# Filler work placed around the first scores and their maxima, divisions one cell later, one cell less for each cross-attention

## The chip, the core and the metric

The kernel runs on one core of a Trainium2 chip. A core has five engines with in-order queues of their own: TensorE (PE; its weight loads are listed as PEld), VectorE (DVE), ScalarE (ACT), GpSimd (POOL) and SyncE (SP, which here only issues DMAs). They meet through semaphores. The metric is the device time of one execution in microseconds (us), lower is better. A second number that matters for TensorE is the clock that it was granted, which the profile gives as a share of full speed.

## What is computed

Two transformer blocks on x, 2 sequences of 1024 tokens with 256 features, all in float32. Heads are 16 wide, 16 of them.

```python
q = ln(x);  x = x + mha(q, q)                 # layer 0: self-attention with biases
x = x + mha(ln(x), ln(ctx))                   # cross-attention to 64 context tokens
h = ln(x); top-2 of 8 experts, gates = softmax # mixture of experts, 1024 hidden units
x = x + sum_k gate_k * expert_k(h)
x = x + sa(ln(x))                             # layer 1: self-attention
x = x + ca(ln(x), ctx, mask)                  # masked cross-attention
x = x + fc2(gelu(fc1(ln(x))))                 # feed-forward
```

## The kernel before

**Cells.** Self-attention of a layer is cut into 128 cells (2 sequences, 2 halves of the queries, 4 groups of 4 heads, 8 blocks of keys; line 899). A cell works on four heads at a time, each in its own 32 rows of the array. It makes two kinds of scores. The "a" scores (L747) have the queries on the partitions and serve only to find each row's maximum (VectorE's reduction, L754). The "b" scores (L758) have the keys on the partitions, with the maximum already folded into the moving operand QB; ScalarE takes their exponential (L764), and `product` (L809) multiplies them with the values, some cells later, for one or two cells at once. ScalarE copies the product out of PSUM into one of two `part` buffers (L821), and POOL adds it to `acc` (L822; VectorE does in the last ten cells, where there are no more maxima). The a scores run `LEAD` = 10 cells ahead. After eight of them `collect` (L782) gathers the maxima, and `largest` transposes them (L702) and subtracts them from the queries (L704, the QB of the group).

**The first ten cells.** In layer 0 nothing precedes the a scores of cells 0 to 9, so they stand alone (`early`, L769), and other work is taken in between. `fill_up(cell, most)` (L784) takes steps from the planner until their cost is used up; `owed` grows by an amount after each early cell and is spent in the same way. Steps that are there to be taken are values (`values`, L594 and the copy L601), keys and queries of the next heads (`project_heads`, L624 and L631, whose rows then travel by DMA, L640), the folded biases (`fold_bias`, L452 to L456, copied by L581 and added to x by POOL, L418) and the context's keys and values (`context_task`: statistics, roots on POOL, centering L346, transposes L358, projections L975 and L997). In layer 1 the early cells are mixed with expert work.

**The planner.** `Stream` holds tasks as generators. A yielded positive number is a cost in us of TensorE; a number at or below zero is a wait, which in the cells is rounded up to whole cells of `CELL` = 2.9 us by setting the task's `first` (L145). Among tasks that may go, the one with the earliest due cell goes. When the cells are over, `rest` (L176) issues what is left, by rank, on a clock of its own that starts at 0, and its table `ready` of when each task may go on starts empty.

**After a pair of head groups.** `finish` sends the sums and the products to DRAM, `gather` fetches the products back, one cell later VectorE inverts the sums (L486) and one DMA writes them out, two cells later another DMA spreads them (L489), three cells later `divide` multiplies (L497, on POOL while there are a scores, else on VectorE), and for the second pair the projection (L426, L434) is added to the stream a cell after that. A quarter of the tokens is a unit; its projection starts a chain of cross-attention (`cross_tasks`: norm, `weigh`, `share`) and, in layer 0, the dispatch to the experts (`dispatch_task`: statistics L332, roots, centering L1255, transposes L358, router L1268, top-2 on VectorE). Expert slots (`slot`, L1592 and L1622) that are known by then fill the rest of layer 0. In `weigh`, as long as there are a scores, scores (SC), maxima (LA), transposes with exponentials (TU), products (PR) and division (DI) are set out by hand over cells (L1170), each line of the list being one cell. Else a second list is used.

PSUM has eight banks, handed out in turn (`bank`, L228), each given back when the engine that drains it has been issued.

Of the kernel before, what the change touches and what calls it, by code (L numbers as in the profile page):

```python
# [61 lines left out]
LEAD = 10  # L62
# [66 lines left out]
class Stream:  # L129
# [46 lines left out]
    def rest(self, later, cell, mark=None):  # L176

        now, ready = 0.0, {}  # L180
        while (self.tasks or later) and (mark is None or mark not in self.made):
            for c in sorted(later):
                if (c - cell) * CELL <= now:
                    for go in later.pop(c):
                        go()
            tasks = [t for t in self.tasks if self.made.issuperset(t.after)]
            able = [t for t in tasks if ready.get(t, 0.0) <= now]
            if able:
                t = max(able, key=lambda t: (t.rank, -ready.get(t, 0.0)))
                cost = self.advance(t)  # L190
                if cost is not None:
                    now += max(0.0, cost)
                    ready[t] = now - min(0.0, cost)
            else:
                now = min([ready[t] for t in tasks] + [(c - cell) * CELL for c in later])
        return now
# [3 lines left out]
def two_blocks(  # L200
# [314 lines left out]
    def self_attention(layer, tail, heads, arrive, extra, when_ready, beside=None):  # L515
# [30 lines left out]
        def at_cell(cell, go):  # L546
            later.setdefault(cell, []).append(go)
# [160 lines left out]
        def finish(h, cell):  # L708
# [11 lines left out]
            if g % 2 == 1:  # L720
                by = opool.tile([P, 512], F32, tag="by", name=f"by_{names}{h}", bufs=1)
                gather(n, dst)
                at_cell(cell + 1, lambda: invert(n, sm))
                at_cell(cell + 2, lambda: spread_out(n, by))
                at_cell(cell + 3, lambda: divide(dst, by))
                if g == 3:
                    at_cell(cell + 4, lambda: project(b, qh))

        def project(b, qh):
            def go():  # L730
# [148 lines left out]
        add_values(1, 34, [("norm", 1)] + (["filled"] if layer == 0 else []))  # L879
        if layer == 0:  # L880

            fill_up(-LEAD, 2.0)
            owed = 0.0
            for ahead in range(0, LEAD, 2):
                cell = now[0] = ahead - LEAD
                for n, _ in enumerate(early(ahead)):
                    for go in later.pop(cell + n, []):
                        go()
                    if (ahead, n) == (6, 1):
                        collect(0)  # L890
                        stream.add(largest(0), 0.75, last=cell, mark=("QB", 0))
                        fill_up(cell, 1.0)
                        stream.until(("QB", 0))

                    owed += 0.7
                    while owed > 0.6 and (cost := stream.step(cell)):
                        owed -= cost
        owed = 0.0
# [143 lines left out]
    def weigh(layer, b, pool, w, name, held):  # L1042
# [124 lines left out]
        SC, LA, TU, PR, DI = scores, largest, weights_turned, product, divided  # L1167
        if maxima[0]:

            for now in (  # L1170
                ((SC, 0, 0), (LA, 0, 0)),
                ((LA, 0, 1),),
                ((SC, 0, 1), (LA, 0, 2)),
                ((TU, 0, 0), (LA, 0, 3)),
                ((SC, 1, 0), (LA, 1, 0)),
                ((TU, 0, 1), (LA, 1, 1)),
                ((PR, 0),),
                ((SC, 1, 1), (LA, 1, 2)),
                ((TU, 1, 0), (LA, 1, 3)),
                ((DI, 0),),  # L1180
                ((TU, 1, 1),),
                ((PR, 1),),
            ):
                for step, *args in now:
                    step(*args)
                us = {SC: cost, TU: 1.15, PR: 1.1, DI: 0.55}.get(now[0][0])
                if us:
                    yield us
                yield 0.0
            return  # L1190
        for step, *args, wait in (
            (SC, 0, 0, None),
# [886 lines left out]
```

## Time and profile before

| | us |
|---|---|
| three timed runs | 1633.61, 1641.87, 1643.48 (median 1641.87) |
| profiled execution | 1630.99 |
| its span, first to last instruction | 1629.2 |
| PE busy in the span | 1581.6 |
| DVE, ACT, POOL busy in the span | 982.0, 912.3, 415.0 |
| mean granted TensorE clock | 0.980 |

The profile is one execution, and its line numbers are those of the kernel before. A row of the timeline gives start, length, engine, line, operation, what is written and what is read, how many instructions were merged (float32 matmuls are recorded twice each), and in brackets how long the engine had been idle and what ended that. A row of waits gives who waited for whom, total, number of times, longest. A row of windows gives the busy time of each engine in a stretch, then the clock, the DMA share and GB/s. A busy PE can also be a matmul that is waiting in the pipeline, since the ends of matmuls are modelled.

A few groups, for scale:

| line, engine, what | count | mean ns |
|---|---|---|
| L754 DVE, maximum of a 128x512 block | 1024 | 682 |
| L764 ACT, exponential of 128x512 | 1024 | 607 |
| L747 PE, a scores | 2048 | 634 |
| L758 PE, b scores | 2048 | 621 |
| L822 POOL, sum of 128x512 | 143 | 1271 |
| L821 ACT, copy of 128x512 | 157 | 597 |

### The profile page before, as it was taken

The numbers are of one execution on the slowest core, as the hardware profiler recorded it, in microseconds if no ns is written. First come the engines' busy times: TensorE is split into PE (matmuls) and PEld (weight loads), VectorE is DVE, ScalarE is ACT, GpSimd is POOL, SyncE is SP. The second block draws the span as 40 slices with busy tenths as digits, with TensorE's granted clock in tenths as the row PEclk, the third lists the DMA queues.
The fourth block names the chain that finished last, engine by engine and source line by source line (L and its number), as shares of the span: only waits on it lengthen the run. The fifth ranks groups of instructions, "written<-read, shape, count | busy, mean of one in ns | idle before, by whom it ended". The sixth has DMA issues, their size and how long they took to land.

```text
span 1629.2 us, 28274 instructions
## 1 busy us (share of the span) xinstructions
PE 1581.6 (97%) x10682; PEld 871.1 (53%) x10682; DVE 982.0 (60%) x2092; ACT 912.3 (56%) x1768; POOL 415.0 (25%) x549
## 2 busy tenths in 40 slices
PE   7999999999999988999999999999999999999998
PEld 3333344444443445788888753344444435536766
DVE  5687857688787737531114467876776877755400
ACT  2376867667665763433322327876776676674321
POOL 2134324234433403041112032411322323321010
PEclk8899999999997998999999999999999999999999
DMA  4333510110100215186566321000110002000000
GB/s 143 124 132 114 180 37 21 27 32 28 36 21 21 67 57 195 62 283 216 175 204 241 92 67 33 24 26 17 36 40 21 21 14 83 15 14 21 14 13 26
DMA packets 56591, 122.09 MB, mean 75 GB/s; under 512 B 12546, under 2 KB 26756, under 8 KB 56068
## 3 DMA queue, kind: packets, MB, share of 16 engines
q1 hardware_dynamic: 52612, 110.08, 20.9%
q0 software_dynamic: 3456, 9.51, 1.6%
q8 instruction: 86, 1.41, 0.4%
q10 hardware_dynamic: 384, 0.66, 0.2%
q14 instruction: 53, 0.43, 0.1%
HBM read 72.14 MB, written 39.42 MB: 68 GB/s over the span
## 4 chain that ended last, share of the span: by engine, by line
PE 91%; DVE 6%; issue 1%; DMA 1%; ACT 1%; POOL 0%; SPq 0%; DVEq 0%; POOLq 0%; ACTq 0%
PE banks L758 17%; PE banks L747 15%; PE banks L809 14%; PE banks L1592 8%; PE banks L1622 8%; PE banks L624 4%; PE banks L1764 3%; PE banks L1752 3%; PE banks L426 3%; PE banks L1051 2%; PE banks L594 2%; PE banks L1081 2%; PE banks L1117 2%; DVE mx_s L754 2%; PE banks L358 1%
## 5 line engine op out<-in xcount | busy, mean ns | idle before, releaser
L754 DVE TENSOR_REDUCE mx_s<-banks 128x1 f32<-128x512 f32 x1024 | 634.6, 682 | 209.3 <-PE banks L747 204.1
L764 ACT ACTIVATE pt_s<-banks 128x512 f32<-128x512 f32 x1024 | 531.2, 607 | 153.0 <-PE banks L747 127.5
L747 PE MATMUL banks<-KS,QS 16*128 16x512 f32 x2048 | 537.6, 634 | 3.5 <-issue 1.9
L758 PE MATMUL banks<-qb_s,KS 32*128 32x512 f32 x2048 | 511.7, 621 | 7.5 <-DVE qb_s L704 4.2
L822 POOL TENSOR_TENSOR acc_s<-acc_s,part_s 128x512 f32<-128x512 f32 x143 | 181.8, 1271 | 426.0 <-ACT part_s L821 414.0
L758 PEld LDWEIGHTS banks<-qb_s,KS 32*128 32x128 f32 x2048 | 177.8, 186 | 181.4 <-DVE mx_s L754 104.4
L809 PE MATMUL banks<-pt_s,v_s 128*20 128x512 f32 x2048 | 262.3, 605 | 0.7 <-DVE sc_c L1102 0.5
L747 PEld LDWEIGHTS banks<-KS,QS 16*128 16x128 f32 x2048 | 198.6, 187 | 77.2 <-issue 37.1
L1622 PE MATMUL banks<-w_slot,h_s 128*128 128x256 f32 x640 | 143.1, 380 | 0.0
L809 PEld LDWEIGHTS banks<-pt_s,v_s 128*20 128x20 f32 x2048 | 42.5, 98 | 181.2 <-ACT pt_s L764 128.9
L1622 PEld LDWEIGHTS banks<-w_slot,h_s 128*128 128x128 f32 x640 | 120.7, 190 | 19.8 <-DVE mx_s L754 1.5
L821 ACT COPY part_s<-banks 128x512 f32<-128x512 f32 x157 | 93.7, 597 | 62.0 <-PE banks L809 51.5
L1631 DVE SCALAR_TENSOR_TENSOR ys<-banks,gate,b 128x256 f32<-128x256 f32 x40 | 19.3, 483 | 162.8 <-PE banks L1622 161.6
L1598 ACT ACTIVATE h_s<-banks,w_slot 128x256 f32<-128x256 f32 x104 | 43.7, 471 | 119.3 <-issue 65.7
L1637 POOL DMA_INDIRECT results<-ys,to x40 | 38.6, 964 | 252.9 <-DVE ys L1631 169.3
L1592 PE MATMUL banks<-xsT,w_slot 128*128 128x256 f32 x416 | 95.7, 381 | 0.7 <-ACT xsT L365 0.7
L1592 PEld LDWEIGHTS banks<-xsT,w_slot 128*128 128x128 f32 x416 | 77.3, 190 | 14.8 <-DVE mx_s L754 2.3
L624 PE MATMUL banks<-xT_s,w_att 128*128 128x512 f32 x128 | 68.6, 672 | 0.0
L1755 ACT ACTIVATE h_f<-banks,w_ff 128x512 f32<-128x512 f32 x32 | 22.0, 687 | 73.9 <-PE banks L1752 73.9
L1102 POOL TENSOR_TENSOR sc_c<-sc_c,mx_c 128x512 f32<-128x512 f32 x38 | 39.5, 1042 | 76.9 <-DVE mx_c L1101 76.9
L1764 PE MATMUL banks<-w_ff,h_f 128*128 128x256 f32 x256 | 57.3, 380 | 0.0
L1752 PE MATMUL banks<-hT_f,w_ff 128*128 128x512 f32 x128 | 56.3, 593 | 0.0
(260 smaller groups left out, 1609.6 us busy)
## 6 DMA issues: line engine op xcount, KB each, us to landing
w_slot<-in_ff_w_dram SPq DMA_DIRECT2D x40, 576.0 KB
sorted_rows<-fill SPq DMA_DIRECT2D x36, 520.0 KB
w_slot<-in_ff_w_dram SPq DMA_DIRECT2D x26, 514.0 KB
whole<-acc_s SPq DMA_DIRECT2D x32, 256.0 KB
spare<-in_ff_w_dram SPq DMA_DIRECT2D x14, 514.0 KB
xs<-sorted_rows SPq DMA_DIRECT2D x20, 260.0 KB
ot_s<-whole SPq DMA_DIRECT2D x16, 256.0 KB
by_s<-turns SPq DMA_DIRECT2D x16, 256.0 KB
```

Source lines behind the costliest of these rows:

```text
L624: nc.tensor.matmul(p, lhsT=w[:, at + k * D + pair * P : at + k * D + (pair + 1) * P], rhs=xT[b][:, k, blk * 512 : (blk + 1) * 512], start= ...
L747: nc.tensor.matmul(sc, lhsT=QS[h % 4][r, qc * P : (qc + 1) * P], rhs=K[r, kh * 512 : (kh + 1) * 512], start=True, stop=True,)
L754: return i, lambda: nc.vector.tensor_reduce(mx[h][:, qc, j, kh : kh + 1], sc, AX.X, ALU.max)
L758: nc.tensor.matmul(sc, lhsT=K[r, n * P : (n + 1) * P], rhs=QB[h][r, :], start=True, stop=True)
L764: nc.scalar.activation(pt, sc, AF.Exp, scale=SCALE)
L809: nc.tensor.matmul(o[32 * j : 32 * j + VW, :], lhsT=V[b][:, cell % 8, 4 * g + j, :], rhs=exps.pop((cell, j)), start=(cell == cells[0]), st ...
L821: nc.scalar.copy(part, o)
L822: helper().tensor_tensor(acc[h], acc[h], part, ALU.add)
L1592: nc.tensor.matmul(ph[:, n, :], lhsT=w[:, at : at + P], rhs=xT[:, k, :], start=(k == 0), stop=(k == 1),)
L1622: nc.tensor.matmul(py, lhsT=h1[:, f, h * P : (h + 1) * P], rhs=w[:, f * D : (f + 1) * D], start=(f == 0), stop=(f == 7),)
L1752: nc.tensor.matmul(ph, lhsT=w1[:, at : at + P], rhs=hT[:, k, :], start=(k == 0), stop=(k == 1))
L1764: nc.tensor.matmul(py[:, n, :], lhsT=h1[:, f, t * P : (t + 1) * P], rhs=w2[:, f * D : (f + 1) * D], start=(f == 0), stop=(f == 7),)
```

## The change

Five edits. The table `ready` of `rest` starts from each task's `first`, so that a wait begun in the cells goes on in the rest. The division comes four cells after `finish` instead of three while there are a scores, and the projection after it moves along. Before the first score, steps worth 4 us are taken instead of 2; after each early cell 1.4 us are owed instead of 0.7; and after the first `collect`, up to 3 us of steps are taken ahead of the transposes of the maxima, and up to 1 us behind them. The hand-set list of `weigh` has eleven entries instead of twelve: the second scores of the second group come ahead of the first product, one maximum goes beside the product, and the first division beside the last transposes. Its cost is the sum over the entry's steps instead of the first step's alone, and if the a scores have ended while it runs, the waits written in the list are used instead of a cell.

```diff
-        now, ready = 0.0, {}
+        now, ready = 0.0, {t: (t.first - cell) * CELL for t in self.tasks}
...
-                at_cell(cell + 3, lambda: divide(dst, by))
+
+                late = 3 + maxima[0]
+                at_cell(cell + late, lambda: divide(dst, by))
                 if g == 3:
-                    at_cell(cell + 4, lambda: project(b, qh))
+                    at_cell(cell + late + 1, lambda: project(b, qh))
...
-            fill_up(-LEAD, 2.0)
+            fill_up(-LEAD, 4.0)
             owed = 0.0
             for ahead in range(0, LEAD, 2):
                 cell = now[0] = ahead - LEAD
...
                     if (ahead, n) == (6, 1):
                         collect(0)
+                        fill_up(cell, 3.0)
                         stream.add(largest(0), 0.75, last=cell, mark=("QB", 0))
+                        stream.until(("QB", 0))
                         fill_up(cell, 1.0)
-                        stream.until(("QB", 0))
-
-                    owed += 0.7
+
+                    owed += 1.4
                     while owed > 0.6 and (cost := stream.step(cell)):
                         owed -= cost
...
-            for now in (
-                ((SC, 0, 0), (LA, 0, 0)),
-                ((LA, 0, 1),),
-                ((SC, 0, 1), (LA, 0, 2)),
-                ((TU, 0, 0), (LA, 0, 3)),
-                ((SC, 1, 0), (LA, 1, 0)),
-                ((TU, 0, 1), (LA, 1, 1)),
-                ((PR, 0),),
-                ((SC, 1, 1), (LA, 1, 2)),
-                ((TU, 1, 0), (LA, 1, 3)),
-                ((DI, 0),),
-                ((TU, 1, 1),),
-                ((PR, 1),),
-            ):
+            for now, wait in (
+                (((SC, 0, 0), (LA, 0, 0)), 0.0),
+                (((LA, 0, 1),), 0.0),
+                (((SC, 0, 1), (LA, 0, 2)), 0.0),
+                (((TU, 0, 0), (LA, 0, 3)), 0.0),
+                (((SC, 1, 0), (LA, 1, 0)), 0.0),
+                (((TU, 0, 1), (LA, 1, 1)), 0.0),
+                (((SC, 1, 1), (LA, 1, 2)), 0.0),
+                (((PR, 0), (LA, 1, 3)), -1.5),
+                (((TU, 1, 0),), None),
+                (((DI, 0), (TU, 1, 1)), -1.4),
+                (((PR, 1),), None),
+            ):
                 for step, *args in now:
                     step(*args)
-                us = {SC: cost, TU: 1.15, PR: 1.1, DI: 0.55}.get(now[0][0])
+                us = sum({SC: cost, TU: 1.15, PR: 1.1, DI: 0.55}.get(step[0], 0.0) for step in now)
                 if us:
                     yield us
-                yield 0.0
+                if maxima[0]:
+                    yield 0.0
+                elif wait is not None:
+                    yield wait
```

## The prediction

> **What bounds the kernel now.** The page comes first: TensorE is busy for 97% of the span and the chain that ended last is 91% PE. So only two things can shorten the run: TensorE's idle time, and time in which its clock is granted at less than full. The span times (1 - 0.980), its mean clock, is 32.6 us; idle is 1629.2 - 1581.6 = 47.6 us.
>
> ```profile
> PE 1581.6 (97%) x10682; PEld 871.1 (53%) x10682; DVE 982.0 (60%) x2092; ACT 912.3 (56%) x1768; POOL 415.0 (25%) x549
> PE 91%; DVE 6%; issue 1%; DMA 1%; ACT 1%; POOL 0%; SPq 0%; DVEq 0%; POOLq 0%; ACTq 0%
> ```
>
> Next the windows, to find where both lie (columns: window, length, busy time of PE, PEld, DVE, ACT, POOL, then the clock):
>
> ```profile
> 20.00:30.00 10.00, 8.10 (x29) 4.84 (x32) 2.48 (x4) 1.22 (x3) 0.00 (x0) 0.83 0.35 67
> 30.00:40.00 10.00, 10.00 (x36) 3.69 (x33) 7.27 (x12) 0.69 (x1) 0.00 (x0) 0.66 0.01 2
> 40.00:50.00 10.00, 9.95 (x28) 3.01 (x24) 7.29 (x13) 0.69 (x1) 0.00 (x0) 0.66 0.00 0
> 50.00:60.00 10.00, 7.26 (x20) 2.74 (x24) 5.82 (x10) 0.48 (x1) 0.00 (x0) 0.66 0.33 52
> 155.00:160.00 5.00, 5.00 (x20) 1.24 (x16) 1.60 (x3) 1.70 (x4) 1.26 (x1) 0.63 0.00 0
> 504.00:508.00 4.00, 4.00 (x21) 0.81 (x22) 3.79 (x13) 1.55 (x4) 1.31 (x7) 0.50 0.00 0
> 600.00:604.00 4.00, 2.21 (x10) 2.09 (x11) 3.45 (x18) 1.06 (x3) 0.00 (x0) 0.50 0.35 125
> 636.00:640.00 4.00, 4.00 (x6) 1.33 (x4) 0.00 (x0) 0.69 (x1) 0.00 (x0) 0.50 1.04 396
> ```
>
> Full clock reigns nearly everywhere else. The first scores (20 to 60 us) are the worst place: VectorE's reductions pace them, yet VectorE itself is busy only 73%, because at half clock the projections between them take twice as long, 3.71 us a pair against 1.91 later. Then the waits of PE, and the timeline around 146 us:
>
> ```profile
> PE banks L358 <- DVE xd_m L1255: 5.4, 1, 5.4
> PE banks L702 <- DVE spread L782: 2.8, 1, 2.8
> 146.64 1.27 POOL L497 TENSOR_TENSOR ot_s<-ot_s,by_s 128x512 f32<-128x512 f32 x1 [7.59 <-DMA by_s<-turns]
> 149.16 0.59 ACT L821 COPY part_s<-banks 128x512 f32<-128x512 f32 x1 [3.27 <-POOL acc_s L822]
> 149.80 1.13 PE L747 MATMUL banks<-KS,QS 16*128 16x512 f32 x4 [1.58 <-ACT part_s L821]
> ```
>
> The last three read as a chain: POOL stands 7.59 us at the division, three partial sums queue behind it, ScalarE finds no free part buffer, and TensorE stops for 1.58 us. The clock then drops (0.69 and 0.63 in the next two windows of 5 us).
>
> **Part 1: work around the first scores.** No instruction is added or removed; they move. In the built order, both first pairs of values now stand before the first score: 1.9 us more of PE work where PE sat idle 1.9 us for the DMA into KS (22.96 start). Both end at 22.96, so it costs nothing. Then each of cells 0 to 2 is followed by a pair of projections; after cells 4 and 7 a value pair, after 5 and 6 a bias fold.
> At full clock: a cell's scores 1.07 us, a pair of projections 1.91, values 1.92, both bias folds 3.15; VectorE needs 2.48 for a cell. VectorE's first cell runs 24.1 to 26.6, as now. Cell 1 can start at 27.9 (scores of cell 0 end at 25.5, plus 1.91), cell 2 at 30.9, cell 3 at 33.8; then TensorE is ahead and VectorE paces: cell 7 ends at 33.8 + 5 x 2.48 + 0.42 (bias copy) = 46.6, the collect at 46.8, transposes (0.6) at 47.4. TensorE's last filler ends near 43.9, so it waits 2.9 there as now (2.8). The scores of cells 8 and 9 follow, and the first paired cell starts at 49.5. It starts at 60.5 now: 11.0 gained. In front of it stand also two value tasks and the biases that now come after (2 x 1.92 + 3.15 = 7.0), which TensorE, at 100% from 60 to 80, needs no longer there. Against that, the first two paired cells are paced by VectorE at 2.48 instead of 1.94: -1.1. Ideal: 17.
> The clock is the unknown. At its present mean there (0.65 to 0.70) the 20 us of TensorE work from 25.5 to the collect become some 30, the paired cells start at 54 to 56, and 10 is left. If VectorE also never starves, 20. I take 16: from 25.5 to 33.3 TensorE has no gap, which is when rows of 35.9 to 39.2 regained full clock, and after it there are 3 us of slack for two half-clock spells of 3.4 us.
> The row behind that doubt: from 29.1 to 34.8 PE shows busy without a gap, and the clock still fell near 32.4, while score matmuls waited for banks. The Trainium skill ("TensorE: Matmul & The Clock Gate", Part 1) has the clock halve after an idle window of about 3.4 us that runs free, and advises against gaps over about 3 us; by that alone this stage would stay at full clock and the gain would be the ideal one. The spacing agrees (changes near 25.7, 29.1, 32.4, 39.2, 42.6, 49.5, 52.9), the condition does not, since no such idle gap stands before 32.4; I follow the row.
> What travels along: 16 key and query DMAs on SP (0.62 us each by the 4.96 for eight) come some 14 us earlier and pass nothing, as the fills start only with cell 2. ScalarE's copies (0.59 to 0.69) fall where it idles 8.8 us and more. POOL gets four bias sums (4.95) and fourteen small root steps (3.8) in a row, from 44 to 53; before it idled 53 us. The one new wait: VectorE's two context centerings stand behind the reductions of cells 8 to 10, near 55.5, and need those roots; behind them queue the reductions of cell 11 and so TensorE's banks. Margin 2 us, cost 0, bound 3; without the margin each us is lost once.
>
> **Part 2: division a cell later.** The wait of 7.59 shrinks by one cell of 2.9 to 4.7, and one more partial sum passes in front. Two sums then queue, which two part buffers hold; the third copy is due at 148.7 and its buffer frees at 147.9 + 1.25 = 149.15, so ScalarE is 0.45 late where 3.27 late cost TensorE 1.58. Gain: 1.6 idle plus the half clock after (1.5 in the window 150 to 155, 1.85 in the next): 5.0, bounds 1.6 and 5. The other nine waiting divisions show no PE wait, so nothing. The projection behind each division (PE 3.65, VectorE 2 x 0.69) comes a cell later, beside other cells: 0.
>
> **Part 3: fewer cells for cross-attention, and waits kept into the rest.** The sum of work is unchanged; what counts is when unit 2 is through. In the built order layer 0's unit 2 is about two cells ahead at the end of the cells, so its centered rows are issued before the last cell ends instead of after. The 5.4 us wait of L358 goes, with the low clock behind it (600 to 608: 2.21 x 0.5 + 4 x 0.23 = 2.0). What is late next: the last cells then have less filler, and ScalarE paces them at 2.06 + 0.6 = 2.66 against TensorE's 2.05, 0.6 for four cells = 2.4; and about 1 us between the transposes and the router, where slot 0 no longer stands. 5.4 + 2.0 - 2.4 - 1.0 = 4.0; bounds 1 and 7.4. In layer 1 and in its tail the order of the rest is the same: 0.
> At 504 to 520 a PE wait of 1.4 us was followed by 17 us at half clock: 9.9 us in all. VectorE there has 3.1, 2.4 and 1.0 us of extra work in three successive cells (hot-one steps of the dispatch with the norm's statistics); now the statistics come a cell later: 2.0, 2.4, 2.1. The same sum, more evenly: 0 to 9.9, I take 4.
>
> **The sum.** 16 + 5 + 4 + 4 = 29. The profiled execution took 1630.99 (span 1629.2 and 1.8 around it): 1602. The three timed runs have their median 10.9 above that and their lowest 2.6 above; I add 5: **1607**. Lower bounds 10 + 1.6 + 1 + 0 = 12.6 with the full 10.9 give 1629; upper bounds 20 + 5 + 7.4 + 9.9 = 42.3 with 2.6 give 1591.
>
> **Rivals.** (a) The first scores gain almost nothing: a halved clock feeds on itself. At half clock throughout, TensorE's work from 25.7 to the first paired cell, 22 us, takes 44 and ends near 69, 8.5 late, which the 7.0 moved work just pays for; the other parts leave 13, less 1.5: 1620 plus 5 = 1625. For it: the clock was low in two thirds of this stage with filler between the scores. Against: filler is what regained it, at 39.2 and 49.5. (b) The 5.4 and 1.6 us waits return elsewhere, since both come from chains, not from TensorE: 16 + 4 remain, 1616. (c) Slower: the small waits on VectorE around each dispatch of layer 0 (cells 68 to 114) turn into half-clock spells like that at 504, 9.9 us each. For it: the dispatch of unit 0 and the norm of unit 1 move against each other there. Against: the same work at the first dispatch costs 0.2 us now. Three such spells eat the gain, five make it 1630.99 + 5 - 29 + 49.5 = 1657. (d) That the change does not do what it says is excluded by the built order.
>
> **How the numbers follow.** Forecast 0.68, (a) 0.15, (b) 0.12, (c) 0.05. A measurement tells about 1% (16 us, so 1625.5 and 1658.3) from no change. Forecast and (b) fall below 1625.5 but for a tenth, (a) for less than half: faster 0.78; slower 0.04, as (c) sits at its limit; the same 0.18. Range 1591 to 1628.
>
> **What would show it.** The first L758 matmul near 49.5 (wrong beyond 56), clock above 0.85 from 25 to 50; no PE wait on part_s near 125 and the division's wait under 5.5 us; no L358 wait on xd_m near 570; TensorE's mean clock 0.985 or more. Wrong altogether if the clock rows show more half-clock time than now while the waits are gone.

## The result, and the profile after

The changed kernel takes 1637.63 us (median of 12 runs, 1631.01 to 1640.61), the kernel before, measured with it, 1638.17 (12 runs, 1632.43 to 1643.48). The ratio is 0.9984, 95% interval 0.9965 to 1.0003: no change that can be told, where 1607 was forecast. The profiled execution of the changed kernel took 1637.98 us, span 1636.2. That is close to its median; the profiled execution of the kernel before (1630.99) lies below all of its 12 runs, so the 7 us by which the profiles differ are not there in the medians.

The head of the page (busy time, share and instructions of each engine; then the chain that ended last, by engine):

```profile
PE 1586.0 (97%) x10682; PEld 877.8 (54%) x10682; DVE 980.7 (60%) x2094; ACT 912.4 (56%) x1766; POOL 410.5 (25%) x545
PE 88%; DVE 8%; DMA 2%; issue 1%; ACT 1%; another core or an unknown queue 0%; SPq 0%; POOL 0%; DVEq 0%; POOLq 0%; ACTq 0%
```

TensorE is about as busy as before, and its mean clock is 0.978 instead of 0.980. Where, the windows say (window, length, busy PE, PEld, DVE, ACT, POOL, then the clock):

```profile
20.00:30.00 10.00, 9.87 (x37) 4.92 (x35) 3.95 (x7) 1.78 (x4) 0.00 (x0) 1.00 0.35 67
30.00:40.00 10.00, 10.00 (x52) 4.90 (x54) 9.00 (x16) 1.96 (x3) 0.00 (x0) 1.00 0.38 64
40.00:50.00 10.00, 8.90 (x53) 5.05 (x50) 9.80 (x21) 1.87 (x2) 5.25 (x6) 1.00 0.76 292
50.00:60.00 10.00, 10.00 (x36) 6.76 (x35) 9.22 (x17) 4.77 (x8) 2.47 (x13) 0.61 0.38 151
60.00:70.00 10.00, 10.00 (x56) 4.63 (x58) 3.06 (x5) 5.28 (x11) 0.00 (x0) 0.71 0.01 2
140.00:150.00 10.00, 10.00 (x44) 3.31 (x44) 2.64 (x5) 4.18 (x8) 2.53 (x2) 0.61 0.00 0
400.00:405.00 5.00, 5.00 (x25) 1.64 (x23) 4.13 (x8) 2.76 (x6) 1.04 (x1) 0.54 0.17 56
526.00:530.00 4.00, 4.00 (x17) 2.03 (x20) 3.47 (x9) 1.19 (x3) 3.06 (x3) 0.50 0.15 54
```

The first scores now run at full clock with VectorE at 90 to 98%, as forecast, but the clock is lost right behind them, from 52 to 66 us. The half clock of 503 to 520 is gone from its place, and new stretches stand at 400 to 407 and 523 to 533, where the kernel before had full clock. The list of PE's waits, and the timeline around the first division (line numbers are 2 to 5 higher than before: L749 is the a scores, L823 ScalarE's copy of the product, L824 GpSimd's sum):

```profile
PE banks L358 <- DVE xd_m L1260: 3.3, 1, 3.3
PE banks L749 <- ACT part_s L823: 1.8, 1, 1.8
```

```profile
133.79 1.27 POOL L497 TENSOR_TENSOR ot_s<-ot_s,by_s 128x512 f32<-128x512 f32 x1 [7.84 <-DMA by_s<-turns]
136.31 0.59 ACT L823 COPY part_s<-banks 128x512 f32<-128x512 f32 x1 [3.52 <-POOL acc_s L824]
136.95 1.52 PE L749 MATMUL banks<-KS,QS 16*128 16x512 f32 x4 [1.83 <-ACT part_s L823]
```

The chain that part 2 was to break stands as it was, link by link: 7.84 us at the division (7.59 before), 3.52 at the copy (3.27), 1.83 at TensorE (1.58).

To compare kernels stage by stage one needs milestones that all of them pass. The 32 subtractions L704, one per group of eight cells, serve: their start times cut the run into pieces, and quiet pieces repeat within 0.1 us from kernel to kernel. Two such rows of the changed kernel's timeline, the 11th and the 12th, 40.6 us apart where the kernel before has 35.3:

```profile
375.10 0.68 DVE L704 TENSOR_TENSOR qb_s<-QS,banks 128x512 f32<-128x512 f32 x1
...
415.66 0.69 DVE L704 TENSOR_TENSOR qb_s<-QS,banks 128x512 f32<-128x512 f32 x1 [0.96 <-PE banks L702]
```

and the same two of the kernel before:

```profile
384.72 0.68 DVE L704 TENSOR_TENSOR qb_s<-QS,banks 128x512 f32<-128x512 f32 x1
...
420.02 0.69 DVE L704 TENSOR_TENSOR qb_s<-QS,banks 128x512 f32<-128x512 f32 x1 [0.74 <-PE banks L702]
```

| piece (numbers of L704) | before | changed | difference |
|---|---|---|---|
| start to 1st | 53.8 | 48.6 | -5.2 |
| 1st to 3rd | 68.5 | 60.6 | -7.9 |
| 3rd to 5th (the first division) | 57.1 | 58.9 | +1.8 |
| 5th to 10th | 170.5 | 170.7 | +0.2 |
| 10th to 14th (dispatch of unit 0, cross-attention of unit 1) | 136.7 | 144.6 | +7.9 |
| 14th to 16th (dispatch of unit 1) | 76.3 | 77.4 | +1.1 |
| 16th to 17th (end of layer 0, all of its rest) | 397.0 | 401.1 | +4.1 |
| 17th to 32nd | 476.7 | 478.8 | +2.1 |
| 32nd to the end | 192.7 | 195.5 | +2.9 |

The sum is +7.0, the difference of the spans. The 13.1 us that the start wins are there, and one stage pays 7.9 of them back. The last two lines are mostly clock: in layer 1 the order of instructions is the same but for details, and there the changed kernel's profile has half-clock stretches of 1.7 to 3.4 lost us (at 967, 1458 and 1520) that the other lacks. The end of layer 0 is not so explained: both profiles spend 17 us at half clock there, and in all kernels that piece varies between 395 and 404 us.

### The profile page after: what moved, and what is told of

Its sections match the earlier page's. It is cut to its first block, busy times and chain, and to the rows that moved or that the text cites. A ratio compares the mean times of both kernels' runs of the same rounds, so it can differ in the third digit from the quotient of the medians.

```text
span 1636.2 us, 28264 instructions
## 1 busy us (share of the span) xinstructions
PE 1586.0 (97%) x10682; PEld 877.8 (54%) x10682; DVE 980.7 (60%) x2094; ACT 912.4 (56%) x1766; POOL 410.5 (25%) x545
## 4 chain that ended last, share of the span: by engine, by line
PE 88%; DVE 8%; DMA 2%; issue 1%; ACT 1%; another core or an unknown queue 0%; SPq 0%; POOL 0%; DVEq 0%; POOLq 0%; ACTq 0%
PE banks L760 16%; PE banks L749 15%; PE banks L811 14%; PE banks L1597 8%; PE banks L1627 8%; PE banks L624 4%; PE banks L1769 3%; PE banks L426 3%; PE banks L1757 3%; DVE mx_s L756 3%; PE banks L1054 2%; PE banks L594 2%; PE banks L1084 2%; PE banks L1120 1%; PE banks L358 1%
## 5 line engine op out<-in xcount | busy, mean ns | idle before, releaser
L749 PE MATMUL banks<-KS,QS 16*128 16x512 f32 x2048 | 538.6, 632 | 3.6 <-ACT part_s L823 1.8
L760 PE MATMUL banks<-qb_s,KS 32*128 32x512 f32 x2048 | 518.7, 625 | 6.4 <-DVE qb_s L704 3.7
L824 POOL TENSOR_TENSOR acc_s<-acc_s,part_s 128x512 f32<-128x512 f32 x141 | 179.4, 1272 | 443.0 <-ACT part_s L823 442.3
L749 PEld LDWEIGHTS banks<-KS,QS 16*128 16x128 f32 x2048 | 200.9, 186 | 74.5 <-issue 35.8
L1627 PE MATMUL banks<-w_slot,h_s 128*128 128x256 f32 x640 | 145.0, 383 | 2.9 <-ACT h_s L1603 2.9
L823 ACT COPY part_s<-banks 128x512 f32<-128x512 f32 x155 | 92.7, 598 | 65.7 <-PE banks L811 55.6
L1597 PEld LDWEIGHTS banks<-xsT,w_slot 128*128 128x128 f32 x416 | 77.3, 190 | 14.8 <-DVE mx_s L756 2.3
L1105 POOL TENSOR_TENSOR sc_c<-sc_c,mx_c 128x512 f32<-128x512 f32 x38 | 40.0, 1054 | 103.0 <-DVE mx_c L1104 103.0
L1760 ACT ACTIVATE h_f<-banks,w_ff 128x512 f32<-128x512 f32 x32 | 22.0, 687 | 73.9 <-PE banks L1757 73.9
L624 PE MATMUL banks<-xT_s,w_att 128*128 128x512 f32 x128 | 62.5, 623 | 0.0
L1603 ACT ACTIVATE h_s<-banks,spare 128x256 f32<-128x256 f32 x56 | 23.4, 471 | 61.9 <-issue 31.3
```

Source lines behind the costliest of these rows:

```text
L624: nc.tensor.matmul(p, lhsT=w[:, at + k * D + pair * P : at + k * D + (pair + 1) * P], rhs=xT[b][:, k, blk * 512 : (blk + 1) * 512], start= ...
L749: nc.tensor.matmul(sc, lhsT=QS[h % 4][r, qc * P : (qc + 1) * P], rhs=K[r, kh * 512 : (kh + 1) * 512], start=True, stop=True,)
L760: nc.tensor.matmul(sc, lhsT=K[r, n * P : (n + 1) * P], rhs=QB[h][r, :], start=True, stop=True)
L823: nc.scalar.copy(part, o)
L824: helper().tensor_tensor(acc[h], acc[h], part, ALU.add)
L1597: nc.tensor.matmul(ph[:, n, :], lhsT=w[:, at : at + P], rhs=xT[:, k, :], start=(k == 0), stop=(k == 1),)
```

## The experiments

Three theories stood at the start. M: the new order of divisions and cross-attention gives back what the start wins. W: stalls meet the clock by chance wherever they fall, so that a lead does not last. S: the slow clock of the first scores is only moved behind them. Each ratio below is to the kernel before in the same session, with its 95% interval.

**The parts one by one.** Kernel before plus part 1 (the fills and the 1.4 owed); plus part 2 (`late = 3 + maxima[0]`); plus part 3 (the list of eleven entries, and `ready`); plus 2 and 3.

> Kernel before with part 1 alone (4.0 and 3.0 us of filler, 1.4 owed). Kernel before has its median near 1638. The full change led by 13 us at the subtraction of the third group's maxima (near 109 us) and had lost all of it by 962 us. Theory M (the new order of divisions and cross-attention gives back what the start wins): the lead of 8 to 13 us is kept to the end, 1625 to 1630. Theory W (stalls of 1 to 3 us meet the clock by chance wherever they fall, so that a lead does not last): lead of 8 to 13 us near 110 us, and an end of 1633 to 1640 with half-clock spells at places where the kernel before has none. Theory S (the slow clock of the first scores is only moved behind them): lead under 6 us near 110 us, 1632 to 1638.

> Kernel before with the division a cell later alone. Theory M: the work that piles up behind a later division costs 3 to 6 us, 1641 to 1644, visible as longer waits of POOL for the spread sums and more waits of TensorE. Theory W: 1634 to 1642, no sign that can be told beforehand. By the prediction's own term: the 1.6 us wait on the part buffers near 150 us goes, 1633.

> Kernel before with the shorter hand list of cross-attention and the waits kept into the rest. Theory M: 3 to 6 us slower, 1641 to 1644, with new half-clock spells beside cells of cross-attention. Theory W: 1634 to 1642. By the prediction's own terms (5.4 us wait at the end of layer 0, spell at 504 to 520): 1630.

> Parts 2 and 3 together without part 1. Theory M: 1645 to 1650, since with part 1's 8 to 13 us the full change ends level with the kernel before. Theory W and theory S: 1634 to 1642, and its difference from the kernel before is not the sum of the differences that parts 2 and 3 show alone.

| | median us | ratio | 1st L704 | 1st to 3rd | 10th to 14th | 14th to 16th |
|---|---|---|---|---|---|---|
| part 1 | 1629.56 | 0.9954 (0.9923 to 0.9984) | 51.0 | 60.4 | 137.5 | 77.5 |
| part 2 | 1640.34 | 1.0026 (0.9996 to 1.0056) | 53.9 | 68.5 | 142.4 | 73.9 |
| part 3 | 1646.31 | 1.0047 (1.0023 to 1.0072) | 51.0 | 68.2 | 145.0 | 74.3 |
| parts 2 and 3 | 1647.59 | 1.0051 (1.0026 to 1.0076) | 55.0 | 68.5 | 144.6 | 77.3 |

The median of the kernel before was 1638.19 here. Part 1 gains 8.6 us, parts 2 and 3 together lose 9.4, and the two cancel: theory M. Part 3 loses 8.1 by itself, more than the 3 to 6 that M had given it; part 2's interval still holds no change. The stage is the same in the three kernels with part 2 or 3: 5.7 to 8.3 us more than the 136.7 of the kernel before, from the 10th to the 14th L704. With part 2 the piece from the 11th to the 12th is 40.2, 40.7 and 40.6 us (part 2, parts 2 and 3, changed kernel), against 35.3 in the kernel before and 36.2 in part 1. In part 3 alone that piece is 36.4, and the loss stands one piece earlier (40.3 against 34.8).

What is in that piece: the dispatch of unit 0 (the top-2 in many small steps on VectorE, then eight scatter DMAs that GpSimd issues) and the norm and first scores of the next cross-attention. The traces show that the two moved against each other. Counted in cells of a scores by VectorE's maxima, the top-2 stands in cells 88 and 89 in the kernel before and in 87 and 88 in the changed one, the scatter in 92 to 95 and in 91 to 93; the four centerings L346 of the next norm stand in 87 and 88 and in 88 and 89. So the dispatch came a cell earlier and the norm a cell later, and the centerings now fall behind the top-2's second half.

By an estimate of VectorE's backlog, cell by cell from the built order and the mean durations (VectorE's work less TensorE's, summed up, not below 0), it reaches 3.7 us at the 89th cell in the changed kernel, 3.1 in part 3 alone and 2.2 at most in the kernel before. The estimate takes 0.58 us for a centering, its mean over the run; the rows in this place show 0.41, so it is somewhat high. The next edit moved the top-2's second half away.

**The top-2's second half three cells later.** In the dispatch:

```diff
-            yield -1.0
+            yield -10.0 if maxima[0] and k == 0 else -1.0
```

on the changed kernel, on part 1 alone, and on the kernel before.

> The changed kernel, with the second half of the dispatch's top-2 (from the second maximum on) three cells later, so that the norm's centering for the next cross-attention (four L346 of 0.58 us) no longer falls into the same two cells. Backlog of VectorE, worked out cell by cell from the built order and the mean durations of the profile before (VectorE's work less TensorE's, not below 0): peak near the 89th cell of a scores 3.7 us in the changed kernel, 0.3 here; 2.2 in the kernel before. Theory M (backlog over about 3 us starves TensorE of PSUM banks, and the clock halves for a window or more): the 400 to 412 us spell goes, the stretch from the tenth to the fourteenth L704 falls from 144.7 us (changed kernel) to 137 to 139, and the whole from 1637.6 to about 1631. Theory W (chance): no change of the stretch that can be told, 1634 to 1641.

> Part 1 alone, with the same delay in the dispatch. In part 1 alone no backlog over 2.2 us stands near the 89th cell, but 3.8 to 6.2 us at the 116th to 121st (spell at 515 to 522 us); here the peak there is 3.6. Theory M: the stretch from the 14th to the 16th L704 falls from 77.6 to 73 or 74 us, and the whole from 1629.6 to 1625. Theory W: 1627 to 1633, the spell at another place.

> The kernel before with nothing but the delay in the dispatch (second half of the top-2 three cells later). It says what the three parts of the change are worth once VectorE's backlog of the dispatch is out of the way: the changed kernel with the delay was 0.989 of the kernel before, part 1 alone with the delay 0.992. Theory M: the spell of 17 us at 504 to 520 goes (stretch from the 14th to the 16th L704 72 to 73 instead of 76.3), the stretch from the 10th to the 14th stays at 137, the whole is 4 to 6 us below the kernel before (0.997), so that parts 1 to 3 together are worth 12 to 14 us on top. Theory W: within 2 us of the kernel before.

| | median us | ratio | 10th to 14th | 14th to 16th |
|---|---|---|---|---|
| changed, with the delay | 1615.84 | 0.9892 (0.9866 to 0.9919) | 137.4 | 69.5 |
| part 1, with the delay | 1620.00 | 0.9923 (0.9898 to 0.9948) | 137.9 | 72.1 |
| before, with the delay | 1644.23 | 1.0020 (0.9995 to 1.0045) | 139.6 | 79.0 |

The medians of the kernel before were 1632.98 for the first two and 1637.97 for the third. One line turns a change of -0.2% into one of -1.1%, more than was expected of it (the stage falls from 144.6 to 137.4, and the next one from 77.4 to 69.5). On the kernel before it gains nothing, which was a miss: there is no collision at the 89th cell to undo, the stage is 2.9 us longer (probably because the top-2's later steps fall beside the cross-attention's maxima, which was not tested), and the half clock of 503 to 520 was expected to go and did not.

Those two last kernels show how much is chance. In the cells of the 14th to 16th L704 they have the same order on VectorE, ScalarE and GpSimd and the same waits of TensorE (1.4 us on the maxima, 1.4 on a centering), and yet (windows of part 1 with the delay, then of the kernel before with it):

```profile
505.00:515.00 10.00, 8.41 (x64) 3.92 (x61) 9.69 (x27) 6.80 (x13) 3.81 (x3) 1.00 0.01 2
515.00:525.00 10.00, 10.00 (x54) 4.03 (x57) 6.50 (x19) 6.03 (x13) 4.78 (x5) 1.00 0.10 37
```

```profile
500.00:510.00 10.00, 8.61 (x48) 2.77 (x47) 8.56 (x21) 5.23 (x10) 3.67 (x14) 0.76 0.07 27
510.00:520.00 10.00, 10.00 (x64) 2.74 (x56) 6.13 (x12) 6.14 (x13) 3.72 (x5) 0.72 0.00 0
520.00:530.00 10.00, 8.41 (x42) 3.40 (x39) 8.12 (x22) 4.53 (x10) 2.86 (x3) 0.66 0.01 2
```

The first keeps the full clock and passes in 72.1 us, the second loses it twice and takes 79.0.

**Backlog or scatter?** The delay moves the top-2's steps and also the scatter behind them. The changed kernel with the scatter's last steps alone three cells later (`yield -10.0 if maxima[0] else -1.5` ahead of the addresses; the top-2 and the centerings stay together), and part 3 alone with the delay of the top-2:

> The changed kernel, with only the last steps of the dispatch (the slots' addresses on VectorE, 0.57 us twice, and the eight scatter DMAs of GpSimd behind them) three cells later; the top-2 and the centering stay together, backlog 3.7 us at the 89th cell and 3.8 to 5.2 at the 117th to 121st as in the changed kernel. If the backlog is the cause: intervals to the 11th and 12th L704 36.3 and 40 as now, half clock near 400, the whole 1636 to 1639. If the scatter is the cause of the second: the interval to the 11th stays 36.3, the one to the 12th falls from 40.6 to 35 or 36, and the whole is 1628 to 1633.

> Part 3 alone with the top-2's second half three cells later. Part 3 alone: 145.0 us from the 10th to the 14th L704, 1.0047 of the kernel before. If its loss is the same collision: 137 to 139, ratio 0.997 to 1.000. If part 3 costs by itself (its cells hold more steps): 142 to 145, ratio 1.003 to 1.006.

The first: 1619.99 us, ratio 0.9938 (0.9913 to 0.9963; kernel before 1630.73). The piece to the 11th L704 stays at 36.3, so the backlog by itself costs 1.5 (34.8 in the kernel before). The piece to the 12th falls from 40.6 to 35.5: of the 7.9 us, the scatter was the larger part. The next stage is 69.8 instead of 77.4, but how much of that is the edit's can't be told: the four profiles of the changed kernel with the top-2's delay have 69.5, 70.4, 72.9 and 75.1 there. In the medians the later scatter alone brings about half of what the delay brings (0.9984 to 0.9938, against 0.9892). The kernel before has the group's last sum ahead of the scatter:

```profile
395.25 1.29 POOL L822 TENSOR_TENSOR acc_s<-acc_s,part_s 128x512 f32<-128x512 f32 x1 [9.38 <-ACT ga_m L1335]
...
400.63 1.21 POOL L1365 DMA_INDIRECT sorted_rows<-xd_m,at_m  x1 [2.12 <-DVE at_m L1357]
```

The timeline of the changed kernel:

```profile
383.81 1.21 POOL L1370 DMA_INDIRECT sorted_rows<-xd_m,at_m  x1 [5.35 <-DVE at_m L1362]
...
387.59 1.27 POOL L824 TENSOR_TENSOR acc_s<-acc_s,part_s 128x512 f32<-128x512 f32 x1
...
395.67 0.96 POOL L1370 DMA_INDIRECT sorted_rows<-xd_m,at_m  x1 [0.30 <-issue]
396.65 2.05 POOL L1105 TENSOR_TENSOR sc_c<-sc_c,mx_c 128x512 f32<-128x512 f32 x2
```

```profile
392.89 1.91 PE L811 MATMUL banks<-pt_s,v_s 128*20 128x512 f32 x16
396.27 0.59 ACT L820 COPY acc_s<-banks 128x512 f32<-128x512 f32 x1 [2.51 <-PE banks L749]
```

and of the kernel with the later scatter:

```profile
380.69 1.26 POOL L824 TENSOR_TENSOR acc_s<-acc_s,part_s 128x512 f32<-128x512 f32 x1 [6.13 <-ACT part_s L823]
...
390.74 0.58 ACT L820 COPY acc_s<-banks 128x512 f32<-128x512 f32 x1 [1.11 <-PE banks L811]
395.37 1.21 POOL L1370 DMA_INDIRECT sorted_rows<-xd_m,at_m  x1 [3.38 <-DVE at_m L1362]
```

Each scatter DMA takes GpSimd 0.96 to 1.21 us, with one every 1.3 us or so. In the changed kernel the last sum of the group stands behind three of them (its part was copied at 384.5, the sum ran at 387.6), and the cross-attention's subtractions L1105 behind all eight. ScalarE's first copy of the next group, L820, runs 1.5 us after the end of its product (392.89 + 1.91 = 394.80, an end that the profile models); with the later scatter it follows at once. The row names TensorE as what ended ScalarE's wait, and TensorE's semaphore, on which the copy waits last, has no step between 392.53 and 396.25 us: it is TensorE's signal that comes late. VectorE then stands idle for 2.6 us, until 397.77, and 400 to 407 is half clock. In part 2 alone and in parts 2 and 3 the same copy is 1.4 and 2.3 us late, so it is not one odd execution. How the scatter leads to it is not shown: in part 3 alone seven of the eight scatter DMAs stand ahead of the group's last sum, and L820 follows its product at once.

Part 3 with the delay: 1633.25 us, ratio 1.0013 (0.9999 to 1.0027), 140.1 us in the stage instead of 145.0, half clock at 380 to 387 gone. That lies between the two expectations (137 to 139, 142 to 145): about 5 of part 3's 8 us there are the collision; the other 3 were not traced.

**The wait on the part buffers.** Part 2 was to remove it and did not. A third buffer removes it without a change in the order of instructions (the room comes from five small VectorE tiles with one buffer instead of two):

```diff
-                part = opool.tile([P, 512], F32, tag="part", name=f"part_{names}{cells[0]}")
+                part = opool.tile([P, 512], F32, tag="part", name=f"part_{names}{cells[0]}", bufs=3)
```

> The kernel before with three part buffers instead of two (five small VectorE tiles go from two buffers to one for the room); every engine's order is that of the kernel before. The prediction put the removal of TensorE's wait on part_s at 5.0 us, bounds 1.6 and 5. The interval from the 4th to the 5th L704 has been 29.4 to 34.9 in twelve profiles with the wait, 27.2 in the two with three buffers. Expected: 27.2 here too, ratio 0.996 to 0.998. Rival: GpSimd's late sums hold something else in this order, 29 to 33, ratio 1.

> The changed kernel with three part buffers, nothing else. Expected: interval 27.2, and 4 to 7 us below the changed kernel, ratio 0.994 to 0.996 where the changed kernel was 0.9984.

> The changed kernel with the delay in the dispatch, and three part buffers instead of two (five small VectorE tiles go from two buffers to one for the room); the order of instructions is the same on every engine. This tests the prediction's price for the wait that part 2 was to remove: TensorE's wait on part_s near 135 us (1.2 to 1.8 in all kernels that have it) with one to three half-clock windows behind it. The interval from the 4th to the 5th L704 is 31.1 to 34.9 with it and 27.1 in the one kernel that lacked it. If the wait is the cause: interval 27 to 29, the whole 4 to 7 us below the changed kernel with the delay alone (1615.8 where the kernel before has 1633; ratio 0.989), ratio 0.985 to 0.987. Rival: the wait moves to TensorE's next one, since GpSimd's three sums still end 3.96 us after the division: interval 31 to 34, ratio 0.988 to 0.990.

| three buffers on | median us | ratio | 4th to 5th L704 |
|---|---|---|---|
| the kernel before | 1623.49 | 0.9956 (0.9938 to 0.9974) | 27.2 |
| the changed kernel | 1622.36 | 0.9945 (0.9926 to 0.9964) | 27.2 |
| the changed kernel with the top-2's delay | 1615.68 | 0.9872 (0.9836 to 0.9908) | 27.2 |

With two buffers that piece took 29.4 to 34.9 us in the 14 profiles that have the wait of 1.2 to 1.8 (mean 32.5), and 27.1 in the one that lacks it (the kernel of the next experiment). So the wait and the half clock behind it cost 5.3 on average, and 2.2 to 7.7 in single executions. The kernel before with three buffers, around its first division (GpSimd's division, with its wait as long as ever; then windows):

```profile
147.32 1.27 POOL L497 TENSOR_TENSOR ot_s<-ot_s,by_s 128x512 f32<-128x512 f32 x1 [7.52 <-DMA by_s<-turns]
148.55 6.66 POOL L822 TENSOR_TENSOR acc_s<-acc_s,part_s 128x512 f32<-128x512 f32 x5
```

```profile
148.00:152.00 4.00, 4.00 (x40) 1.22 (x36) 3.36 (x6) 3.45 (x7) 3.84 (x4) 1.00 0.99 400
152.00:156.00 4.00, 4.00 (x24) 1.52 (x20) 1.65 (x4) 2.46 (x6) 3.05 (x3) 1.00 0.13 53
```

GpSimd stands as long, and the sums queue behind the division as before (now five without a pause, since their parts have come in time); nobody waits for them, and the clock stays. The third of these kernels has the fastest profile of the study (1610.42 us, mean clock 0.991), but its 0.9872 can't be told from the 0.9892 of the delay alone: beside the delay the buffer's gain shows in the piece and not in the whole.

One thing came unasked: with the third buffer on the changed kernel, the piece to the 12th L704 was 35.5 although the scatter stood where it was. Both kernels were profiled once more.

> The changed kernel as it is, profiled once more. If the stall near 396 us belongs to it: interval from the 11th to the 12th L704 40 to 41 again, ScalarE's L820 there released 1.4 to 2.3 us after the product's end. If it comes by chance: 35 to 36. In both cases the interval to the 5th L704 is 29 to 35, with 0 to 3 windows of half clock behind the same wait of 1.2 to 1.8.

> The changed kernel with three part buffers, profiled once more. If the third buffer takes the stall near 390 us away: 35.5 again. If it was missing by chance: about 40. The interval to the 5th L704 is 27.2 again.

The changed kernel again: 1636.05 us, piece 40.3, L820 released at 396.41 with the same idle time (2.53). With three buffers again: 1627.36 us, piece 36.5, L820 0.6 us late. So the stall belongs to the changed kernel, and either edit relieves it. The copy waits for TensorE; what holds TensorE's signal back was not found, and that stays open. One lead, not tested: in three of the four executions with the stall (the changed kernel twice and part 2 alone) a 16 KB load of instructions by DMA ends 0.02 to 0.05 us before the signal, in the fourth 0.7 us before it; in five executions with an edit that relieves it, it begins 0.3 us before the signal to 1.3 us after it.

**What VectorE's time costs TensorE.** Extra maxima of a constant in four quiet cells of the kernel before, whose result nobody reads:

```diff
+            for n in range(doses.get((layer, cell), 0)):
+                nc.vector.tensor_reduce(extra_mx, picks[:, :512]..., AX.X, ALU.max)
```

> The kernel before with extra maxima of 128x512 (about 0.68 us each) on VectorE, whose result nobody reads, in four quiet cells: 5 in cell 18 and 6 in cell 34 of layer 0, 4 in cell 18 and 9 in cell 25 of layer 1. Peak backlogs by the same count: 2.8, 3.5, 2.1 and 5.5 us. The intervals between successive L704 there repeat within 0.1 us in all kernels so far (24.0, 26.6, 24.0 and 27.9 us). Theory M: 2.1 costs nothing, 2.8 nothing to 0.5, 3.5 about 0.5 to 1 plus perhaps half a window of clock (1.7), 5.5 costs 2.5 plus one or two windows (1.7 to 3.4). Theory W: cost without relation to the size, by where the window happens to stand; a stall of under 1 us may cost 1.7 or 5, one of 2.5 may cost no clock.

The rows of the second and fourth place (VectorE's extra work; who waited, total, times, longest; and the windows right behind):

```profile
194.23 4.28 DVE L916 TENSOR_REDUCE dose<-picks 128x4 f32<-128x512 f32 x6
...
1063.67 6.44 DVE L916 TENSOR_REDUCE dose<-picks 128x4 f32<-128x512 f32 x9
```

```profile
PE banks L759 <- DVE mx_s L755: 2.7, 1, 2.7
...
PE banks L759 <- DVE mx_s L755: 4.8, 1, 4.8
```

```profile
200.00:204.00 4.00, 4.00 (x20) 1.44 (x20) 2.79 (x6) 1.45 (x3) 0.00 (x0) 0.50 0.37 136
...
1070.00:1074.00 4.00, 3.24 (x14) 2.02 (x16) 3.03 (x6) 1.08 (x2) 0.00 (x0) 0.50 0.01 2
```

| extra on VectorE, in one cell | longest wait of TensorE | piece longer by | of it lost to half clock |
|---|---|---|---|
| 2.84 | 1.2 | 2.2 | 0 |
| 3.56 | 1.9 | 2.9 | 0 |
| 4.28 | 2.7 | 7.9 | 5.1 |
| 6.44 | 4.8 | 7.9 | 3.4 |

Of the two smaller bursts all but 0.65 us is lost, so the expectation (nothing up to 2.1 of backlog) was too kind. That is about a cell's slack there: eight cells take 24.0 us, 3.0 a cell, against VectorE's 2.48; no cushion beyond it shows. Of the two larger bursts 2.8 and 4.5 us are left when the half clock is taken off, so there the two losses overlap and can't be told apart. The half clock comes in steps, and its size does not follow the wait's.

**The first scores.** Two edits on the half clock behind the first QB: part 1 with 1.0 us owed and without the 3.0 us ahead of the first transposes, and the changed kernel with the delay and the context's task not before cell 2 (`first=2`), alone and with the third buffer.

> Part 1 alone, with 1.0 us owed per early cell instead of 1.4 and without the 3.0 us ahead of the first transposes: a value pair stays for the two cells behind the first QB and the context's centering comes three cells later. If the half clock of 54 to 68 us in part 1 alone (3.4 us of work lost twice) comes from VectorE pacing bare cells: it is halved or gone, the second L704 comes 30 to 32 us after the first instead of 34.3, the first one 0 to 2 us later, and the whole is 1626 to 1629. If it comes by chance or from anything else: the interval stays at 34, 1629 to 1632.

> The changed kernel with the delay in the dispatch, and the context's task not before cell 2: its statistics and centering (four steps of 0.41 and 0.18, two of 0.58 us) leave the cells behind the first QB, where VectorE paces, and come 5 cells later. The prediction put their cost at 0, bound 3. If they are part of why the clock halves from 54 to 68 us: the interval from the first to the second L704 falls from 34.4 to 31 to 33, the whole 1 to 3 us below the delay alone. If the half clock comes from the bare cells as such: 34 to 35, no difference over 1 us.

> The two edits together, on the changed kernel with the delay: three part buffers and the later context task. Sum of the two if they are independent, as they lie 70 us apart: ratio 0.983 to 0.987 if both work, 0.988 to 0.990 if neither does.

1626.88 us, ratio 0.9967 (0.9949 to 0.9984); 1618.74, 0.9875 (0.9840 to 0.9910); 1621.43, 0.9895 (0.9861 to 0.9929). The first has its first L704 at 48.1, but 40.6 us to the second, where 30 to 32 was expected, and 66.7 to the third instead of 60.4: the half clock only began earlier (44.8 to 62). In the other two the piece to the second L704 falls to 32.0 and 33.3, which was the sign for the context's steps, but the next piece grows from 26.1 to 30.4 in both; the half clock is where it was (54 to 68, 54 to 70), and the time to the third L704 is 62.4 and 63.7. So the context's centering is not its cause, as the prediction had priced it (0). What is, was not isolated: the cells there are bare, with TensorE's 2.05 us against VectorE's 2.48, and neither edit changed that. The pair of edits (0.9895) falls where the expectation put it if neither works, although its piece from the 4th to the 5th L704 is 27.2: again the third buffer's gain does not show in the whole beside the delay.

## Why the prediction was wrong

Of the 29 us, part 1 brought 8.6; parts 2 and 3, priced at 13 together, cost 9.4. The base was 2 us too low besides: the median of the kernel before is 7.2 above its profiled execution, where 5 was added.

- **Part 1, 16 us (bounds 10 to 20): right in kind, and too high.** Its signs came: the first b scores at 49.95 (49.5 forecast, 60.51 before), full clock from 25 to 50, the wait on `spread` at 1.1 instead of 2.8. Over nine profiles with part 1 the first L704 stands at 50.3 on average (54.5 in eight without), and the next two pieces take 60.6 instead of 68.5: 12 us. In medians part 1 alone gained 8.6 (2.6 to 12.6 by its interval). The term that was off is the clock. The two or more cells behind the first QB, costed at "-1.1" for VectorE's pace, were followed by 13.7 us of half clock (6.8 us of work lost in 52 to 66, and as much in each of the nine profiles). And "from 25.5 to 33.3 TensorE has no gap" held, but did not keep the clock: in six of the nine, the changed kernel's second profile among them, it halves from about 26 to 30, and the first L704 comes at 50.5 to 51.9 instead of 48.4 to 48.6. Theory S is right for that share.
- **Part 2, 5 us: the step "one more partial sum passes in front" failed.** In the built order GpSimd's first division stands behind 13 sums in the kernel before and in part 2 alone, the next four behind 25, 34, 42 and 52 in both; the fourth and fifth move by one only where part 3 is in. The planner issued it a cell later, and the queue did not change; rival (d) had been excluded "by the built order", and for this queue it was what happened. The price was right (5.3 measured by the third buffer); the change did not do the thing priced.
- **"A cell later, beside other cells: 0" for the moved projection, and "the sum of work is unchanged" for part 3: this is the step that cost the forecast.** The projection starts the norm, and a unit's cross-attention ends in the dispatch and its eight GpSimd DMAs. One unit's norm came a cell later and the other's dispatch a cell earlier, which put centerings behind the top-2's second half, and the scatter ahead of the group's last sum and beside the next cross-attention's first scores: 7.9 us between the 10th and the 14th L704. The word "same sum, more evenly" was read for one place, 504 to 520, and not for the other dispatch. For that place 4 was taken; the stage lost 1.1.
- **The end of layer 0, 4 us: not seen.** The wait of 5.4 us shrank to 3.1 to 3.3 in all kernels with part 2 and to 2.1 in the two with part 3 alone (5.3 to 5.4 in those with neither). The piece that holds it takes 395.3 to 401.5 us without parts 2 and 3 (seven profiles, mean 397.7) and 395.6 to 401.1 with both (ten, mean 399.0). A wait 2 us shorter did not make the piece shorter; what took it was not traced, and the spread of the piece is larger than that.
- **The rivals.** Rival (b) had the waits return elsewhere; in fact part 2's stayed in its place and of part 3's more than half is left. The mechanism that ate the rest is nearest to rival (c), waits around the dispatches of layer 0, above all at 395 to 407 (the half clock of 523 to 533 stands for the 17 us of 503 to 520 that went); its ground, that dispatch and norm "move against each other there", is what the cells show. It was given 0.05 because "the same work at the first dispatch costs 0.2 us now", which was true of the old neighbours only, and GpSimd's scatter, which it did not name, was the larger share of it. Of the named signs, those of the first scores came and the others (no wait on part_s, division's wait under 5.5, no wait on xd_m, clock 0.985) failed. The one for "wrong altogether" came by half: there is more half clock over the whole run (mean clock 0.978 against 0.980), but the waits are not gone, and at the first scores there is less of it than before (13.7 us against 23.9).

## What to carry to other kernels

When an edit shifts a chain by a cell, price every instruction at its far end, DMA issues on GpSimd above all, against its new neighbours; "beside other cells" is a price only where the trace shows those cells with room. A call that a planner makes later is not an instruction that stands later in its queue: compare the built queues before counting what it passes. A third buffer took a wait away here without moving anything else, and was worth more than the whole change (0.9956 against 0.9984). The one line that spaces out the dispatch was worth more than that on top of the change (0.9984 to 0.9892), and nothing on the kernel before (1.0020): what such a line is worth depends on the neighbours that the other edits made.

## What the runs showed of the hardware

- **Half clock comes in whole pieces, and how many is not set by the stall.** In quarter-us windows every half-clock stretch away from the start and the end of the run is about 3.4, 7, 10 or 17 us long. The same wait on the part buffers (1.2 to 1.8 us) cost none to three such pieces in 14 profiles (none in two of them), and where the wait is gone, in five profiles with the third buffer and in the kernel with the extra maxima, there is no half clock in that place. The same order and waits at the 14th to 16th L704 cost none and five, and the extra VectorE work none after a wait of 1.9, three after 2.7 and two after 4.8. The Trainium skill ("TensorE: Matmul & The Clock Gate", Part 1) describes a free-running activity window of about 3.4 us and two rates, which agrees with the lengths; its section "HAM oscillation" warns of gaps over about 3.4 us, and here gaps of 1.2 to 1.8 us were enough in 12 of the 14 profiles. Its section "A second HAM failure mode: psum-queue depth-cycling", on short and frequent idle times between groups of matmuls, is nearer to these rows, where matmuls wait for PSUM banks behind VectorE or ScalarE.
- **Two executions of one kernel differ by this.** The changed kernel's two profiles agree within 0.3 us in the stage of the 10th to 14th L704 (144.6 and 144.3) and differ by 1.9 at the part buffers and by 1.8 in the next stage. A gain of one or two pieces of half clock can't be read from one profile; the pieces between milestones without half clock can, to 0.1 us.
